# Cross-attention on one core: a new order of the first loads and products, and new costs and ranks in the planner

## The chip, the cores and the metric

The kernel runs on one core of a Trainium2 chip. The metric is the device time of one execution in microseconds. A core has TensorE (PE in the profile; PEld is its loading of weights), VectorE (DVE), ScalarE (ACT), GpSimd (POOL) and SyncE (SP), each with an instruction queue of its own that runs in the written order and waits on semaphores. SP issues nearly all DMA transfers here, POOL the indirect ones and some small loads. SBUF is the memory on the chip, PSUM the banks into which TensorE writes.

## What is computed

`x` is 2 x 2048 x 640, the context 2 x 128 x 384, all in float32. Cut to what matters:

```python
query = x @ Wq                                   # 8 heads of 80
hs = mha(query, enc @ Wk, enc @ Wv)              # enc: the context's first 124 rows
ca_q1 = einsum('btc,th->bch', ca, Wq_ca)[:, indices, :]   # ca: its last 4 rows
ca_hs1 = mha(ca_q1, x, x)                        # x is key and value
ca_q2 = ca_hs1 @ Wq
ca_hs2 = mha(ca_q2, ca @ Wk_ca, ca @ Wv_ca)
out = (hs + ca_hs2) @ Wout + b_out + x
```

`mha` is softmax attention with 8 heads. `indices` repeats 384 rows over 2048, so the second branch is worked out for 384 rows and gathered at the end.

## The kernel before, in words

The kernel is written by a small planner. Each stage is a Python generator that yields steps (`Do`): an engine, a function that emits the instructions, the events that it waits for, the buffers that it takes (`Room`) and frees. The `Desk` holds a queue of ready steps for each engine and a clock of its own. In `run` (from L167 on) it takes the step that can begin first by its estimate; among those that can begin at once it takes the lowest sum of rank and the price of a change of tile shape (`order` and `change`). What it emits is pinned in this order, so the estimate decides the order of every engine's queue, and nothing of it is left to the chip. The parts of the estimate are:

- `matmul` (L210), `transpose`, and `__getattr__` (L228), which prices a VectorE, ScalarE or GpSimd operation by its largest operand;
- `dma` (L254): an issue of 0.45 us, a transfer time given by the caller on one shared channel, and a tail, `more`, until the data can be used;
- the weights `SWITCH`, `LEAVE` and `ANOTHER` for going between whole 128x128 products and products on parts of the array (L70);
- `RANKS`, a table of offsets for single stages (block 3 of the chain of steps and so on), found by a search outside the kernel.

The work in order of time:

1. Head. `first_loads` loads the first 512 rows of `x` in four transfers of 128 rows (320 KB each), then Wq in five chunks. A chunk is 128 columns' worth of heads; the fifth gathers what is left between the others. `idle_work` multiplies zeros to keep TensorE going. `x_first` copies the fifth columns together on VectorE, transposes the rows on TensorE in groups of four tiles and lets ScalarE or VectorE copy each group to SBUF. `queries(0, ..., True)` then makes three of the five output chunks at once, in five parts, one for each chunk of Wq, each on all 512 rows; it begins when the whole of x's first block is there. The transposes, the zeros and the first query products share four PSUM banks; four more, the `quad`, wait for the adapter's scores.
2. Set-up. `keys`, `values_weights`, `text_values`, `y_weights`, `wq_turned` prepare the weights of both branches.
3. Per block of 512 rows (eight): `x_load`, `yz_block` and `y_rows` for the second branch; `queries_fast` for the query product, in a scheme of seven products of halves in place of eight, for which `sums_of_x` and `sums_of_wq` subtract tiles on POOL or VectorE; `halves_away` and `rest_back`, which carry the fifth chunk through DRAM (tiles `away`, `landing`, `rests`).
4. Per pair of 128-row tiles (16): `text_scores` (tile `sc`), `softmax` (maxima `m`, exponentials and product `p` with `r`, transposed `eb`), `probabilities` through DRAM (`kept`, `pT`), `text_out` (hidden `ph`, output `po`), added to `x_more` or `last_rows` and stored.
5. For each batch the `adapter`: scores `s`, their maxima `mx`, exponentials `ea`, contraction `acc`, then `second`, whose rows an indirect DMA gathers and adds at the end (`add_second`).

The lines that matter for the head:

```python
op = yield Do("PE", turn, [("xlast", (n0 + 3) // NCH)], needs=[(banks, 1)])      # x_first: four transposes
...
op = yield Do("PE", part, [*after, ("wq", i)])       # queries: after is [("x", 0, 0)], the whole block
```

Of the kernel before, what the change touches and what calls it, by code (L numbers as in the profile page):

```python
# [64 lines left out]
class Desk:  # L65
# [4 lines left out]
    WHOLE, SWITCH, LEAVE, ANOTHER = (P, P), 9.7, 11.5, -0.4  # L70
# [15 lines left out]
        "adapter": {1: 1},  # L86
        "chain": {8: -11, 9: -18, 11: 6, 12: -2, 14: -17, 15: -5, 17: 4, 18: 4, 19: 4, 20: 9, 24: -15, 37: -13,
            38: 4, 39: -8, 40: 8, 41: 3, 45: -13, 52: -5, 57: -2, 59: 10, 65: -8, 71: 11, 80: -12, 85: 9,
            87: -11},
        "context": {0: -12},  # L90
        "contract": {0: 5, 1: 12, 2: 12, 3: 9},
        "halves_away": {1: -6, 3: -10, 4: -8},
        "keys": {0: 4},
        "probabilities": {1: -2, 2: -4, 3: 7, 4: 1, 6: -1.4, 8: -4},
        "queries": {0: -4},
        "queries_fast": {3: 10, 4: 3},
        "rest_back": {8: 14, 9: 2},
        "softmax": {3: -7, 12: -11, 13: -2, 20: -18, 22: 6, 23: -14, 25: -3, 27: -12, 28: 6},
        "sums_of_wq": {0: 2},
        "text_scores": {3: -3, 6: 2, 11: 6, 12: 6, 14: 6},  # L100
        "text_values": {0: 8},
        "values_weights": {0: 6},
        "wq_turned": {0: 1},
        "x_load": {1: -12, 6: -6},
        "y_rows": {1: 2, 3: 10, 4: 1, 7: 8},
        "yz_block": {0: -13, 1: -4, 2: -2, 6: 5, 7: 2},
    }

    def __init__(self, tc):
        self.tc, self.nc, self.now, self.spent, self.mode = tc, tc.nc, 0.0, 0.0, None  # L110
        self.free = {e: 0.0 for e in self.ENGINES}
        self.queue = {e: [] for e in self.ENGINES}
        self.events, self.landed, self.channel, self.log, self.begun = {}, 0.0, 0.0, [], {}
# [114 lines left out]
    def __getattr__(self, name):  # L228

        side, _, what = name.partition("_")  # L230
        engine = {"v": self.nc.vector, "a": self.nc.scalar, "g": self.nc.gpsimd}[side]
        base, each = {"v": (0.06, 1.04), "a": (0.13, 0.77), "g": (0.1, 2.1)}[side]
        base += self.MORE.get(name, 0.0)

        def call(*args, **kw):
            self.pin(getattr(engine, what)(*args, **kw))  # L236
# [26 lines left out]
def kernel(  # L263
# [36 lines left out]
    FAST, SPARE, IDLE = 2, 0, 14  # L300
# [18 lines left out]
    ending, late = Room(1), {}  # L319
# [120 lines left out]
    def load_w(name, w, **kw):  # L440

        def go(at):
            w_c[name] = sp.tile([P, NCC, H], F32, tag=f"w{at[0]}", name=f"w_{name}")
            dma(w_c[name], w.rearrange("(c p) n -> p c n", p=P), 3.5)
            return at[0]

        return Do("SP", go, needs=[(weights, 1)], marks=[("w", name)], **kw)

    def first_loads():

        def whole(at):
            t = xrow.tile([P, 4 * H], F32, tag="xz", name="xz")
            rows_of[0] = t.rearrange("p (k n) -> p k n", k=4)

        yield Do("NONE", whole, [], needs=[(staging, 1)])
        for k in range(4):
            yield Do(
                "SP", lambda k=k: dma(rows_of[0][:, k], x[0, k * P : (k + 1) * P, :], (0.3, 0.9, 1.4, 1.1)[k], more=2.3), [],
                marks=[("xrows", k)],
            )  # L460
        for c in range(4):
            yield Do(
                "SP", lambda c=c: dma(wq_sb[:, c, :], Wq[D2 * c + VR : D2 * c + VR + P, :], 0.8), [],
                marks=[("wq", c)],
            )
            if c == 0:
                yield Do("SP", lambda: dma(wqca_sb, Wq_ca, 0.1), [], marks=["wqca"])
                yield Do("SP", lambda: dma(ctx_sb, enc.rearrange("b t c -> t b c"), 1.0), [], marks=["ctx"])
# [53 lines left out]
    def idle_work():  # L522
# [6 lines left out]
        op = yield Do("NONE", lambda at: (bank(at[0], "unread"), at[0]), needs=[(banks, 1)])  # L529
        to, at = op.value  # L530
        for n in range(IDLE):

            def product():
                matmul(to[:, :P], zeros, zeros, start=True, stop=True)

            yield Do("PE", product, [] if n else [op.at], frees=[(banks, at)] if n == IDLE - 1 else [])
# [30 lines left out]
    def x_first():  # L567
# [4 lines left out]
            "NONE", lambda s: slot(s[0], "xt_0_0", [P, 4, NCH, P]), [], needs=[(xslots, 1)]  # L572
        )
        xt[0, 0] = op.value, op.slots[0][0]
        flat = op.value.rearrange("p k c s -> p (k c s)")
# [6 lines left out]
        for n0 in range(0, 4 * NCH, 4):  # L582

            def turn(s, n0=n0):
                pt = bank(s[0], f"pt_x_{n0}")
                for n in range(n0, n0 + 4):
                    k, c = divmod(n, NCH)
                    src = rows_of[0][:, k, D2 * c + VR : D2 * c + VR + P] if c < 4 else last[:, k, :]
                    transpose(pt[:, n % 4 * P : (n % 4 + 1) * P], src, ident)
                return pt  # L590

            op = yield Do("PE", turn, [("xlast", (n0 + 3) // NCH)], needs=[(banks, 1)])
            end = n0 + 4 == 4 * NCH
            yield Fork(
                one(evacuate(
                    flat[:, n0 * P : (n0 + 4) * P], op.value, op.slots[0][0], after=[op.at],
                    marks=[("xpart", n0 // 4)],
                )), 1,
            )
        yield Do(  # L600
            "NONE", lambda: None, [("xpart", n) for n in range(NCH)],
# [311 lines left out]
    def load_wout():  # L913

        by_head = Wout.rearrange("(c j d) n -> j d c n", c=4, j=2)
        for j in range(2):
            yield Do(
                "SP", lambda j=j: dma(wout_sb[VH * j : VH * (j + 1), :4, :], by_head[j, :VH], 2.5),
# [132 lines left out]
    def x_load(b, sb, after):  # L1051
# [8 lines left out]
        for i in range(4):  # L1060
            part = slice(R * i, R * (i + 1))
            d0 = VR + R * i
            yield Do("SP", lambda: dma(most[part], v[:, :, :, d0 : d0 + R], 2.2, 1.3), [])
# [33 lines left out]
    def queries(n, after, first=False):  # L1097

        b, sb = divmod(n, NSB)
        yield Do("NONE", lambda: None, after)  # L1100
# [5 lines left out]
        if first:  # L1106
            yield Do("NONE", room, after, needs=[(qslots, 1)])
# [3 lines left out]
            for i in range(NCH):  # L1111

                def part(i=i):
                    for c in range(3):
                        matmul(
                            pq[c], wq_of(i, c), t[:, :, i, :], start=(i == 0), stop=(i == NCH - 1)
                        )

                op = yield Do("PE", part, [*after, ("wq", i)])
# [236 lines left out]
    def halves_away(n, pq, s, at, first=None):  # L1356

        away = away_of[n] = hbm.tile([P, 2, 512], F32, tag=f"rest_{n}", name=f"away_{n}")
        for k in range(2):
            cols, needs, frees = slice(2 * P * k, 2 * P * (k + 1)), [], []  # L1360
            if n:
# [9 lines left out]
                "SP", lambda k=k, z=z, cols=cols: dma(away[:, :, cols], z.bitcast(F32), 0.6), [op.at],  # L1371
# [34 lines left out]
    def yz_block(b, sb):  # L1406
# [35 lines left out]
        for u in range(2):  # L1442
# [10 lines left out]
            if b:  # L1453
                yield Do(
                    "SP", lambda u=u: dma(away[:, u], zs, 1.0), frees=[(zss, i)],
# [32 lines left out]
    def y_rows(b, sb):  # L1488
# [3 lines left out]
        for u in range(2):  # L1492
# [11 lines left out]
            def away(t=op.value, u=u):  # L1504
                dma(kept[:, :, u, :], t.rearrange("p (a n) -> p a n", a=4), 1.0)
# [179 lines left out]
    def second(b):  # L1685
# [12 lines left out]
        def less():  # L1698
            for ct in range(NCC):
                desk.v_tensor_reduce(  # L1700
# [43 lines left out]
        for ct in range(NCC):  # L1744
            op = yield Do("NONE", lambda e: ea_tile(e[0], f"o2_{b}_{ct}"), [here], needs=[(eas, 1)])
            o2, k = op.value.rearrange("p g k -> p (g k)")[:, :H], op.slots[0][0]
            for u in range(2):
# [16 lines left out]
                "SP", lambda: dma(o2_of[b][ct * P : (ct + 1) * P, :], o2, 1.3),  # L1764
# [64 lines left out]
    def softmax(m, k, sc, s, i, at):  # L1829
# [59 lines left out]
    def probabilities(m):  # L1889
# [9 lines left out]
        for j in range(4):  # L1899
            op = yield Do(  # L1900
                "SP",
                lambda: dma(pT[R * j : R * (j + 1)].rearrange("p i k h a -> p i (k h a)"), by_keys[j], 1.1),
# [76 lines left out]
    def residual(m):  # L1979

        xr = xr_of[m] = []
        for b, st in tiles(m):

            def load(at):
                t = row_of[at[0]]
                dma(t, x[b, st * P : (st + 1) * P, :], 1.3)
# [12 lines left out]
    def add_second(t, b, st):  # L1999
# [6 lines left out]
        desk.spent += 1.9  # L2006
        desk.landed = desk.now + desk.spent + 6.5
# [149 lines left out]
    def stored(m, k, both):  # L2157
# [5 lines left out]
        if gather_last[m] and not desk.known(("o2", b)):  # L2163
            part = hbm.tile([P, H], F32, tag=f"early_{m}_{k}", name=f"early_{b}_{st}")
            op = yield Do("SP", lambda: dma(part, t, 1.3), both, frees=[(rows, i)])
            yield Do("NONE", lambda: None, [op.at, ("o2", b)])

            def load(at, _):
                t = row_of[at[0]]
                dma(t, part, 1.3)  # L2170
# [8 lines left out]
        yield Do("SP", lambda: dma(rows_out, t, 1.3), both, frees=[(rows, i)] + own)  # L2179
# [11 lines left out]
    begin = desk.begin  # L2191
    desk.free["POOL"] = 12.0
    begin(idle_work(), 9)
# [57 lines left out]
```

## Time and profile before

| | us |
|---|---|
| median of 3 runs | 603.02 (602.94 to 606.83) |
| the profiled execution, its own time | 603.33 |
| its span, first to last instruction | 601.6 |
| TensorE busy | 583.4 |
| VectorE busy | 405.0 |
| ScalarE busy | 280.7 |
| GpSimd busy | 152.3 |
| end of the last product in the timeline | 597.9 |

A row of a group names the line, the engine, the operation, what it writes and reads, its shape and its count; L211, L221, L236 and L256 are lines of helpers, so groups are told apart by their tiles. A row of waits gives the total, the number and the longest. In the chain of work that ended last each piece is followed back to what released it. In a table of stretches the columns are the stretch, its length, the busy time of PE, PEld, DVE, ACT and POOL with the number of instructions, TensorE's granted clock (1.00 throughout), the DMA engines' busy share and GB/s. One float32 product of a 512-row tile is two instructions.

### The profile page before, as it was taken

How to read it: one execution, taken by the hardware profiler on the slowest of the kernel's cores; microseconds unless marked ns; L12 is line 12 of the kernel's file. 1: busy time of each engine (PE TensorE's matmuls, PEld its weight loads, DVE VectorE, ACT ScalarE, POOL GpSimd, SP SyncE). 2: the span in 40 equal slices, each digit the busy share in tenths (PEclk: the TensorE clock that was granted, in tenths of full speed). 3: DMA queues.
4: the chain of work that ended last, by engine and by line, in shares of the span. 5: the costliest groups of instructions: out<-in, count | busy, mean ns of one | idle time of the engine just before them, and what ended most of it. 6: DMA issues, size and time to landing. Idle time of an engine off the chain costs nothing.

```text
span 601.6 us, 11824 instructions
## 1 busy us (share of the span) xinstructions
PE 583.4 (97%) x4535; PEld 362.8 (60%) x4535; DVE 405.0 (67%) x642; ACT 280.7 (47%) x766; POOL 152.3 (25%) x203
## 2 busy tenths in 40 slices
PE   9999989999999999999999999999999999999997
PEld 6475455856757755465665566656555556666764
DVE  2257698989999977465989999998412243344343
ACT  2233156455445589799735252346865831102010
POOL 7201021413222330100204252534022202124242
PEclk9999999999999999999999999999999999999999
DMA  8998825965769586454898789896673794699997
GB/s 276 176 244 172 137 83 168 178 185 168 131 169 210 151 156 190 151 160 141 182 277 231 190 194 292 221 257 157 192 169 60 173 261 100 220 226 295 213 256 185
DMA packets 153106, 114.21 MB, mean 190 GB/s; under 512 B 83285, under 2 KB 125653, under 8 KB 153050
## 3 DMA queue, kind: packets, MB, share of 16 engines
q1 hardware_dynamic: 147418, 102.77, 66.2%
q0 software_dynamic: 5632, 10.69, 10.7%
q8 instruction: 36, 0.59, 0.4%
q14 instruction: 20, 0.16, 0.1%
HBM read 72.22 MB, written 41.21 MB: 189 GB/s over the span
## 4 chain that ended last, share of the span: by engine, by line
PE 61%; DVE 19%; DMA 8%; ACT 6%; issue 3%; SPq 1%; DVEq 0%; ACTq 0%
PE po L211 22%; PE pq L211 13%; PE ph L211 6%; DVE mx L236 6%; PE acc L211 5%; PE s L211 4%; PE sc L211 4%; DMA pT<-kept 3%; ACT ea L236 3%; ACT p L236 2%; DVE m L236 2%; DMA zb<-z 2%; DVE eb L236 2%; DMA kept<-eb 2%; PE pyz L211 2%
## 5 line engine op out<-in xcount | busy, mean ns | idle before, releaser
L236 DVE TENSOR_REDUCE mx<-s 128x4 f32<-128x2048 f32 x48 | 109.1, 2272 | 8.5 <-PE s L211 8.5
L236 ACT ACTIVATE ea<-s 128x2048 f32<-128x2048 f32 x48 | 91.9, 1915 | 23.8 <-PE s L211 23.5
L236 ACT ACTIVATE p<-sc,m 128x124 f32<-128x124 f32 x256 | 90.9, 395 | 24.4 <-DVE m L236 24.1
L211 PE MATMUL pq<-xt,wq_sb 128*128 128x256 f32 (+1 forms) x272 | 86.4, 452 | 2.5 <-DVE q L236 2.3
L211 PE MATMUL po<-wout_sums,hs 128*128 128x320 f32 x256 | 79.3, 441 | 0.4 <-DVE x_more L236 0.4
L211 PE MATMUL po<-wout_sb,hs 128*128 128x320 f32 x248 | 77.0, 440 | 0.0
L236 DVE TENSOR_TENSOR x_more<-x_more,po 128x320 f32<-128x320 f32 x80 | 38.3, 480 | 56.2 <-PE po L211 54.0
L211 PEld LDWEIGHTS pq<-xt,wq_sb 128*128 128x128 f32 x272 | 48.9, 190 | 28.4 <-issue 18.5
L236 POOL TENSOR_TENSOR p<-p,r 128x992 f32<-128x992 f32 x18 | 33.3, 1848 | 124.4 <-DVE r L236 124.4
L211 PEld LDWEIGHTS po<-wout_sums,hs 128*128 128x128 f32 x256 | 46.6, 190 | 24.5 <-issue 5.1
L236 ACT ACTIVATION_READ_ACCUMULATOR p<-sc,m 128x1 f32 x256 | 60.0, 238 | 0.0
L211 PEld LDWEIGHTS po<-wout_sb,hs 128*128 128x128 f32 x248 | 45.5, 190 | 23.2 <-issue 4.3
L236 ACT COPY hs<-ph 128x512 f32<-128x512 f32 (+1 forms) x34 | 18.7, 551 | 74.8 <-PE ph L211 74.8
L2001 POOL DMA_INDIRECT x_more<-o,query x20 | 32.5, 1626 | 77.1 <-DVE x_more L236 60.9
L211 PE MATMUL acc<-ea,y_sb 128*32 128x384 f32 (+2 forms) x768 | 51.4, 385 | 0.0
L211 PE MATMUL ph<-pT,vpad 128*32 128x256 f32 x768 | 46.3, 381 | 2.9 <-DMA pT<-kept 2.0
L236 DVE TENSOR_REDUCE m<-sc 128x4 f32<-128x496 f32 x64 | 40.0, 660 | 13.1 <-PE sc L211 13.0
L236 DVE TENSOR_TENSOR last_rows<-last_rows,po 128x320 f32<-128x320 f32 x48 | 23.2, 485 | 31.4 <-PE po L211 30.8
L236 ACT CAST rests<-landing 128x512 fp32r<-128x512 f32 x30 | 19.4, 648 | 45.5 <-PE sc L211 42.8
L236 DVE STREAM_TRANSPOSE eb<-p 128x1024 f32<-128x1024 f32 x32 | 39.3, 1229 | 1.8 <-DMA kept<-eb 1.6
L211 PEld LDWEIGHTS sc<-kmain,q 64*128 64x128 f32 x512 | 31.8, 187 | 14.2 <-issue 8.8
L211 PE MATMUL pq<-xt,wq 128*128 128x512 f32 x80 | 39.8, 612 | 0.0
(210 smaller groups left out, 798.4 us busy)
## 6 DMA issues: line engine op xcount, KB each, us to landing
kept<-eb SPq DMA_DIRECT2D x32, 512.0 KB, 3.9
pT<-kept SPq DMA_DIRECT2D x64, 256.0 KB, 7.2
landing<-away SPq DMA_DIRECT2D x60, 128.0 KB, 3.5
xi<-in_x_dram SPq DMA_DIRECT2D x28, 256.0 KB, 4.8
x_more<-in_x_dram SPq DMA_DIRECT2D x20, 320.0 KB, 3.9
out_dram<-x_more SPq DMA_DIRECT2D x20, 320.0 KB, 5.5
y<-yt SPq DMA_DIRECT2D x16, 256.0 KB, 3.6
y_sb<-y SPq DMA_DIRECT2D x32, 128.0 KB, 4.1
```

Source lines behind the costliest of these rows:

```text
L211: self.pin(self.nc.tensor.matmul(out, lhsT, rhs, **kw))
L236: self.pin(getattr(engine, what)(*args, **kw))
L2001: desk.pin(nc.gpsimd.indirect_dma_start(out=t, out_offset=None, in_=o2_of[b], in_offset=bass.IndirectOffsetOnAxis(ap=query[:, st : st + 1] ...
```

## The change

The first loads alternate: x rows 0, x rows 1, Wq 0, Wq 1, x rows 2, x rows 3, Wq_ca, the context, Wq 2, Wq 3. The first four banks of the transposes and of the products of zeros become a tile of the `quad` (`early`), which is given back when x's first block is there. `x_first` transposes the four main tiles of one row group as soon as its rows have landed, and the fifth tiles of two row groups together. `queries(0)` makes the parts of Wq 0 and Wq 1 on 256 rows each, first half before second. The products of zeros go from 14 to 10. All else is in the planner: other transfer times and tails, a charge for VectorE operations with two tiles in SBUF that begin while POOL is at work, other weights for changes of shape, a start of 0.8 us for four engines, and a new table of ranks. The diff, cut to its core:

```diff
-    WHOLE, SWITCH, LEAVE, ANOTHER = (P, P), 9.7, 11.5, -0.4
+    WHOLE, SWITCH, LEAVE, ANOTHER = (P, P), 10.9, 10.2, -2
...
-        "softmax": {3: -7, 12: -11, 13: -2, 20: -18, 22: 6, 23: -14, 25: -3, 27: -12, 28: 6},
+        "softmax": {3: -7, 9: 0.2, 10: 14, 12: -11, 13: -4, 18: -18, 19: -7, 20: -2, 25: -3, 28: 6},
...
+        def both(what, args):
+            if what not in ("tensor_tensor", "scalar_tensor_tensor"):
+                return False
+            pair = (args[1], args[2] if what == "tensor_tensor" else args[3])
+            return all(a.space == bass.MemoryType.SB and a.shape[-1] * a.shape[1] >= 96 for a in pair)
...
+            if side == "g":
+                self.port = self.now + self.spent
+            elif side == "v" and both(what, args) and self.port > self.now:
+                self.spent += min(self.port - self.now, 0.9)
...
-    def dma(self, out, in_, us, issue=0.45, more=2.8):
+    def dma(self, out, in_, us, issue=0.45, more=1.5):
...
-    FAST, SPARE, IDLE = 2, 0, 14
+    FAST, SPARE, IDLE = 2, 0, 10
...
+        yield x_rows(0, 0.3)
+        yield x_rows(1, 0.9)
+        yield chunk(0, 1.3, more=2.3)
+        yield chunk(1, 1.1, more=2.3)
+        yield x_rows(2, 1.1)
+        yield x_rows(3, 1.1)
+        yield Do("SP", lambda: dma(wqca_sb, Wq_ca, 0.1, more=2.3), [], marks=["wqca"])
+        yield Do("SP", lambda: dma(ctx_sb, enc.rearrange("b t c -> t b c"), 1.0, more=2.3), [], marks=["ctx"])
+        yield chunk(2, 0.9, more=2.3)
+        yield chunk(3, 0.9, more=2.3)
...
+    def early_banks():
+        op = yield Do("NONE", lambda s: late_sq.tile([P, 4, 512], F32, tag="sq", name="early"), [], needs=[(quad, 1)])
+        early.tile = op.value
+        early.at += [0.0] * 4
+        yield Do("NONE", lambda s: None, [("x", 0, 0)], needs=[(early, 4)], frees=[(quad, 0)])
...
+        for h in range(2):
+            k0 = 2 * h
+            for n, part in enumerate((
+                [(k0, c) for c in range(4)], [(k0 + 1, c) for c in range(4)], [(k0, 4), (k0 + 1, 4)],
+            )):
...
+            for i, h in ((0, 0), (1, 0), (0, 1), (1, 1), *((i, None) for i in range(2, NCH))):
+                u = slice(0, 4) if h is None else slice(2 * h, 2 * h + 2)
...
-            dma(kept_of[m][:, :, k], eb.rearrange("p j h a -> p j (h a)"), 2.1)
+            dma(kept_of[m][:, :, k], eb.rearrange("p j h a -> p j (h a)"), 1.6)
...
-        desk.spent += 1.9
-        desk.landed = desk.now + desk.spent + 6.5
+        desk.spent += 1.0
+        desk.landed = desk.now + desk.spent + 6.3
...
+    for e in ("PE", "ACT", "DVE", "SP"):
+        desk.free[e] = 0.8
```

The tables of the other stages' ranks change in the same way, and the other transfers: loads of weights 3.5 to 2.6, `x_load` 2.2 to 1.5, rows in and out 1.3 to 0.9, `pT` 1.1 to 1.15 with a tail of 1.9, the parts of Wout 2.5 to 1.8; `away` of the rests goes up, 0.6 to 0.8, `y` 1.0 to 1.5.

More of the change, by code (lines that the diff above doesn't have):

```diff
@@ L318 @@
     yts = Room(2)
-    ending, late = Room(1), {}
+    ending, early, late = Room(1), Room(0), {}
     def bank(i, name):
@@ L527, in idle_work @@
         yield Do("DVE", lambda: desk.v_memset(zeros, 0.0), [])
-        op = yield Do("NONE", lambda at: (bank(at[0], "unread"), at[0]), needs=[(banks, 1)])
-        to, at = op.value
+        op = yield Do("NONE", lambda at: at[0], needs=[(early, 1)])
+        to, at = early.tile[:, op.value], op.value
         for n in range(IDLE):
@@ L581, in x_first, with turn @@
             )), 1)
[L582 to L599, printed above, removed]
+        for h in range(2):
[3 more added lines that the diff above has]
+            )):
+                def turn(s, part=part):
+                    pt = early.tile[:, s[0]]
+                    for i, (k, c) in enumerate(part):
+                        src = rows_of[0][:, k, D2 * c + VR : D2 * c + VR + P] if c < 4 else last[:, k, :]
+                        transpose(pt[:, i * P : (i + 1) * P], src, ident)
+                    return pt
+                op = yield Do(
+                    "PE", turn, [("xrows", k0 + n)] if n < 2 else [("xlast", k0), ("xlast", k0 + 1)],
+                    needs=[(early, 1)],
+                )
+                to = xt[0, 0][0][:, k0 + n, :4] if n < 2 else xt[0, 0][0][:, k0 : k0 + 2, 4]
+                src = op.value[:, : len(part) * P].rearrange("p (c s) -> p c s", s=P)
+                yield Fork(one(Do(
+                    EITHER, lambda to=to, src=src: copy(to, src), [op.at], frees=[(early, op.slots[0][0])],
+                    marks=[("xpart", h, n)],
+                )), 1)
         yield Do(
-            "NONE", lambda: None, [("xpart", n) for n in range(NCH)],
+            "NONE", lambda: None, [("xpart", h, n) for h in range(2) for n in range(3)],
             frees=[(first_rows, at), (staging, 0)], marks=[("x", 0, 0)],
@@ L2178, in stored @@
             both = [op.at]
[L2179 removed]
+        yield Do("SP", lambda: dma(rows_out, t, 0.9), both, frees=[(rows, i)] + own)
     blocks = [(b, sb) for b in range(B) for sb in range(NSB)]
```

97 lines of the change are left out of this document (49 added, 48 removed).

## The prediction, made before the result was known

> **What bounds the kernel now.** I read the page's totals first, then the busy time by stretches, then what TensorE waited for, then the chain that ended last, and last the first ten microseconds and the DMA issues. The totals:
>
> ```profile
> PE 583.4 (97%) x4535; PEld 362.8 (60%) x4535; DVE 405.0 (67%) x642; ACT 280.7 (47%) x766; POOL 152.3 (25%) x203
> ```
>
> TensorE has work for all but 18.2 us of the 601.6 us span. By stretches (length, then busy time of PE, PEld, DVE, ACT and POOL):
>
> ```profile
> 0.00:9.50 9.50, 8.15 (x54) 7.48 (x54) 2.90 (x17) 3.53 (x5) 8.53 (x47) 1.00 0.80 271
> 9.50:75.00 65.50, 65.50 (x346) 35.17 (x346) 34.02 (x80) 15.61 (x41) 10.64 (x46) 1.00 0.92 191
> 75.00:180.00 105.00, 101.29 (x654) 66.10 (x653) 98.88 (x131) 54.60 (x207) 27.82 (x20) 1.00 0.63 154
> ...
> 500.00:601.70 101.70, 97.94 (x590) 65.46 (x588) 41.93 (x89) 11.61 (x24) 28.31 (x18) 1.00 0.89 219
> ```
>
> From 9.5 to 75 us TensorE never rests, so a product that starts earlier moves everything up to 75. From 75 to 180 VectorE is busy 94% of the time and TensorE 96%: two engines bind there at once. The last 100 us are products without a gap and a store behind them. What TensorE waited for, in total, times, longest:
>
> ```profile
> PE pq L211 <- DVE q L236: 4.4, 4, 1.6
> PE ph L211 <- DMA pT<-kept: 2.0, 2, 1.2
> PE s L211 <- DVE mx L236: 1.6, 4, 0.6
> PE s L211 <- ACT ea L236: 1.2, 4, 0.7
> PE pt_p L221 <- DVE p2pad L236: 1.1, 1, 1.1
> PE unread L211 <- DVE zeros L236: 1.1, 1, 1.1
> ```
>
> All rows of that answer add to 13.9 us, 1.3 of them in the head (zeros 1.1, x's rows 0.2). So 12.6 us is all that another order could take out of visible waits; VectorE is named for most of it, DMA for only 2.0. Four pieces of the chain explain some of it (start, length, what):
>
> ```profile
> 78.34 1.44 DVE x_sums L236
> 79.78 2.81 DVE wq_sums L236 x2
> ...
> 149.46 1.56 DVE zop L236
> ...
> 325.98 1.63 DVE wout_sums L236
> ```
>
> The groups show what is odd about them (min/median/max in ns):
>
> ```profile
> L236 DVE TENSOR_TENSOR wq_sums<-wq_sb x2: 384/934/1485, 77.3 to 79.7; 128x256 f32<-128x256 f32 x2
> L236 DVE TENSOR_TENSOR wq_sums<-wq_sums,wq_sb x2: 409/947/1485, 81.1 to 84.3; 128x256 f32<-128x256 f32 x2
> L236 DVE TENSOR_TENSOR x_sums<-xt x1: 1519/1519/1519, 78.3 to 78.3; 128x512 f32<-128x512 f32 x1
> ```
>
> The same instruction takes 384 ns or 1485 ns. In the timeline every slow one starts while POOL runs a subtraction or product of two tiles.
>
> **The change, part by part. The head.** SP now issues x rows 0, x rows 1, Wq 0, Wq 1, x rows 2, x rows 3, then Wq_ca, the context, Wq 2 and Wq 3: the same bytes in the same number of issues. Landings go by place in the queue, so I take them from the old occupants. The first landed 3.0 us after its issue at 0.81, at 3.8; the third let VectorE and TensorE go at 6.57 to 6.59; the fourth at 7.72; the fifth (Wq 0, issued at 2.66, 6.0 to landing) at 8.66; the next 320 KB I put 1 us later, at 9.7. Before, the first useful product stood behind all 20 transposes of x and those of Wq_ca:
>
> ```profile
> 9.47 2.84 PE L211 MATMUL pq<-xt,wq_sb 128*128 128x512 f32 x6
> 12.14 0.38 PE L221 MATMUL pt_ctx<-ident,ctx_sb 128*128 128x128 f32 x2
> ```
>
> After it, the products of Wq 0 with half of the rows start when Wq 0 lands, at 6.6 (the transposes of x rows 1, landed before 5.1, and a copy of 0.59 end by 6.4). Each half part is six instructions at half the 0.43 us of a 512-row one, 1.3 us; the two run from 6.6 to 9.2, the second fed by Wq 1 at 7.7. Then come ten transposes at 0.11 (1.1 us), those of Wq_ca (0.5), and the rest of the first five parts: five parts of 2.57 us are 12.85, less 2.6 done, 10.25, with three pairs of context transposes at 0.22, 0.66. That ends at 6.6 + 2.6 + 1.1 + 0.5 + 10.25 + 0.66 = 21.7, plus a gap for x rows 3: landing 9.7, transposes, a copy of 0.6, so 10.8 against 9.2 + 1.1 + 0.5 already filled, 0 to 0.6. Before, the chain has the same work end at 9.54 + 2.77 + 0.22 + 2.58 + 0.22 + 2.58 + 0.22 + 5.15 = 23.3, some 0.2 of it modelled drain, so 23.1. The gain lies between 0.8 and 1.4, and below that if TensorE's written order stands in front of a late landing: down to -0.3. I take 0.9. It is hidden by nothing up to 75; Wq 2 (needed at about 13.5, landed at 12) and the later loads keep their places, the ninth issue still waiting for the first landing. Fewer idle products (10 for 14) cost nothing: they fill the wait before x's rows, which is still there. The early tile of four banks takes over the transposes' banks until x's first block is done, long before the first scores at 52 us need them; its price is nothing, and 0.4 (one bank's evacuation) if that block's last copy is late.
>
> [...]
>
> **VectorE's collisions.** The estimate now charges a two-tile VectorE operation that begins while POOL is busy. Excess in the rows: wq_sums 2 x (1485 - 409) = 2.15 us; x_sums 1519 - 684 = 0.84; the zop row at 149.38, 1.65 against 0.73, 0.92; wout_sums 1714 against some 820 (by the slope from 409 at 256 to 684 at 512 elements), 0.89; 4.8 us together, all four on the chain. What TensorE gets back is bounded by its own waits behind them: 1.60 at 84.41, 0.69 at 156.91, and 0.43 + 0.58 behind the maxima at 329.87 and 339.89, so 3.3 seen, and up to the 4.8 if the 94% busy VectorE passes the rest on. The other end is nothing: the planner may dodge by letting POOL start later. I take 3.0, near the visible waits. With VectorE early, the next limit at 84 us is the softmax's maxima behind the first scores.
>
> [...]
>
> **The other constants and the ranks.** They add no instruction; they decide the order on each queue. DMA terms shrink. Issue 0.45, transfer and tail together, old, new and measured:
>
> ```profile
> kept<-eb SPq DMA_DIRECT2D x32, 512.0 KB, 3.9
> pT<-kept SPq DMA_DIRECT2D x64, 256.0 KB, 7.2
> landing<-away SPq DMA_DIRECT2D x60, 128.0 KB, 3.5
> ...
> y_sb<-y SPq DMA_DIRECT2D x32, 128.0 KB, 4.1
> ```
>
> kept: 5.35, 3.55, 3.9; landing: 3.95, 2.65, 3.5; y_sb: 3.65, 2.35, 4.1 (four in a row share the channel). The old terms were late by 0.5 to 1.5, the new ones are early by 0.4 to 1.7. The indirect gather goes from 1.9 to 1.0, where the tail shows five starts 1.85 apart. The weights for a change of tile shape shift by about 1 among ranks that differ by 10; one costs about 0.19 (in the chain, eight pq products take 1.92 between other shapes and 1.73 between their like), and with three or four kinds of small products, 48 pieces of acc the most regular of them, ten more or fewer are 1.9 us either way, which I set at nothing. For the new ranks as such the trace gives bounds: all remaining visible waits gone, 12.6 - 3.3 = 9.3 us gained; or every one of the 15 landing groups 0.85 too early for its scores, 12.8 us lost. I take nothing between them, as the estimate errs by the same size on either side.
>
> **The sum.** The profiled execution took 603.33 us (span 601.6 and 1.7 around it), 0.3 over the median of 603.02. 603.33 - 0.9 - 3.0 = 599.4; against the median, 599.1 us.
>
> **Rivals.** (1) Slower: the plan runs early. TensorE's queue is in written order; scores stand behind rests, rests behind landing<-away, and if the scores are placed 0.85 us before their data can be there, each of the 15 groups stalls everything behind it. Eleven of 15 give 9.4: 603.0 - 0.9 - 3.0 + 9.4 = 608.5. It decides from five groups on (4.6 x 0.85 = 3.9). For it: the new terms are below every measured landing above. Against it: only 2.0 us of DMA waits today, with rests given out well ahead. (2) Deeper: with waits charged truly, the search removes half of the 9.3 us that is left: 599.1 - 4.7 = 594.4. For it: VectorE's waits have a name and a price now, and the old terms held transfers back. Against it: with PE and DVE both at 94% and over in 75 to 180, filling one wait opens another. (3) Nothing but the head: the collisions move instead of going, 603.0 - 0.9 = 602.1. For it: POOL's subtractions need the same tiles at the same time as VectorE's.
>
> **How the numbers follow.** Forecast 599.1 (range 596 to 602): 0.33. Deeper: 0.27. Head only: 0.14. Slower: 0.26. About 1%, 6 us, is what a measurement of this kernel tells from no change. Under 597.0 lie 0.24 of the deeper case and 0.07 of the forecast, 0.31; over 609.0 lie 0.19 of the slow one; the other 0.50 is within. The range, from the deeper case with nearly all 9.3 us (590) to the slow one with 11 groups and half a microsecond (609), leaves out 0.2.
>
> **What would show it.** In the head: the first product of x and Wq at 6.6 instead of 9.47, and the first five parts done about 0.9 earlier. Collisions: wq_sums all near 400 ns, no x_sums over 700, no wait of TensorE behind q at 84. The slow rival: TensorE's wait on landing or pT above 5 us, or ACT's rests named before sc. Deeper: the waits of TensorE together below 8 us. I am wrong if those waits stay as they are and the time still moves: then changes of shape or hidden stalls inside the products decide, which the busy time does not show.

## The result, and the profile after

| | us |
|---|---|
| before, median of 6 runs | 604.24 (601.87 to 607.49) |
| after, median of 6 runs | 623.58 (622.42 to 625.57) |
| ratio | 1.0318, 95% interval 1.0278 to 1.0358 |
| after, the profiled execution; its span | 623.33; 621.6 |

The change makes the kernel 3.2% slower; 599.1 was forecast, and the range ended at 609. The profiled span grew by 20.0 us. The same stretches as before, up to the longer end (stretch, its length, busy time of PE, PEld, DVE, ACT, POOL, then granted clock, DMA share, GB/s):

```profile
0.00:9.50 9.50, 7.02 (x28) 6.07 (x28) 1.41 (x7) 2.45 (x3) 8.53 (x47) 1.00 0.78 266
9.50:75.00 65.50, 60.66 (x328) 36.66 (x327) 26.12 (x88) 15.92 (x39) 10.45 (x46) 0.95 0.86 181
75.00:180.00 105.00, 103.42 (x654) 64.21 (x653) 102.14 (x128) 51.39 (x195) 27.83 (x21) 1.00 0.69 165
...
350.00:500.00 150.00, 141.40 (x1324) 84.85 (x1323) 91.29 (x133) 77.04 (x194) 46.34 (x38) 0.98 0.80 202
500.00:621.70 121.70, 112.56 (x749) 72.96 (x747) 44.68 (x99) 22.68 (x33) 31.76 (x24) 1.00 0.78 199
```

The row of before for 350 to 500 us:

```profile
350.00:500.00 150.00, 147.00 (x1415) 86.22 (x1408) 89.99 (x143) 79.22 (x167) 41.15 (x34) 1.00 0.80 196
```

Set these beside the stretches shown before. TensorE now rests 1.6 us in 75 to 180, against 3.7: the middle got better. But it rests 4.8 us in 9.5 to 75, where it never had, 8.6 in 350 to 500 (3.0 before) and 9.1 in the last stretch (3.8). Over the span TensorE's rests grew from 18.2 to 30.6, 12.4 us. Its busy time grew from 583.4 to 591.0, 7.6 us, with four product instructions more among 4539 (twelve from the halves, eight fewer of zeros): nearly the same work ran slower, and two rows show a clock under 1.00. What TensorE waited for:

```profile
PE s L210 <- DVE mx L242: 5.2, 2, 3.9
PE ph L210 <- DMA pT<-kept: 3.2, 2, 2.3
PE pt_vca L220 <- ACT vca L242: 3.2, 1, 3.2
PE po L210 <- DVE last_rows L242: 2.7, 1, 2.7
PE po L210 <- POOL hs L242: 1.6, 1, 1.6
...
PE early L220 <- ACT xt L242: 1.4, 2, 0.7
```

Before, the longest single wait was 1.6 us. Now a few long ones stand there, most of them behind operations whose instructions the change leaves as they were.

To place the loss I counted every product at a fixed time by its shape in both traces, and read when each kernel had done the same amount of TensorE's work. After is 5.7 us behind at 22 us, 4.6 at 59, 11.5 at 82. It then catches up to 5.0 at 355. It is 11.0 behind at 378, 14.9 at 433, 14.1 at 595 and 18.9 at its last product. So the middle gained 6.5 us, and four places lost more: the head, 62 to 72, 355 to 433, and the tail.

**The head.** TensorE's timeline of after, with the wait in brackets:

```profile
8.80 0.80 PE L210 MATMUL early<-zeros 128*128 128x128 f32 x2 [0.68 <-ACT xt L242]
10.11 0.80 PE L210 MATMUL early<-zeros 128*128 128x128 f32 x2 [0.52 <-DVE xt L242]
10.70 4.20 PE L210 MATMUL pq<-xt,wq_sb 128*128 128x256 f32 x12
```

Products of zeros wait for copies of x. They have nothing to do with x, but they are written into the tile `early`, and so are the transposes; a write into one of its banks waits for the copy out of another (e1 below takes this away). The first useful product begins at 10.7, not at 6.6, though Wq 0 landed at 6.8, near the forecast. The twelve take 4.2 us, 0.35 apiece.

**62 to 72 us.** ScalarE's and then TensorE's timeline:

```profile
63.56 1.02 ACT L242 CAST krest<-k_parts 128x992 fp32r<-128x992 f32 x1 [6.83 <-DMA k_parts<-k_away]
...
65.63 0.35 ACT L242 COPY vca<-pvca 128x128 f32<-128x128 f32 x2
```

```profile
65.95 0.47 PE L220 MATMUL pt_vca<-ident,vca 128*128 128x128 f32 x1 [3.19 <-ACT vca L242]
```

ScalarE stands in written order at the cast of `krest` until its transfer lands, the copy of `vca` is written behind it, and TensorE stands behind that. Then the clock falls (a stretch of two microseconds; the third number from the end is the granted clock):

```profile
66.00:68.00 2.00, 2.00 (x11) 1.17 (x12) 2.00 (x4) 0.58 (x1) 0.00 (x0) 0.50 0.56 151
```

**355 to 433 us.** VectorE, and TensorE behind it:

```profile
367.16 1.25 DVE L242 STREAM_TRANSPOSE eb<-p 128x1024 f32<-128x1024 f32 x1 [4.75 <-DMA kept<-eb]
368.32 0.16 DVE L242 RECIPROCAL r<-r 128x8 f32<-128x8 f32 x1
368.41 2.24 DVE L242 TENSOR_REDUCE mx<-s 128x4 f32<-128x2048 f32 x1
```

```profile
370.70 0.50 PE L210 MATMUL s<-zop,cop 32*128 32x512 f32 x4 [3.93 <-DVE mx L242]
```

`eb` has one buffer. Its store was issued at 357.05 and landed 10.0 us later, where the median of that group is 3.9. VectorE waits 4.75 for it, the maxima `mx` stand behind, and TensorE's scores behind them.

The late landing itself is not new. In before, the chain that ended last and VectorE's timeline have the same store at this place:

```profile
355.70 11.01 DMA kept<-eb
```

```profile
356.20 2.28 DVE L236 TENSOR_REDUCE mx<-s 128x4 f32<-128x2048 f32 x1
...
360.44 2.29 DVE L236 TENSOR_REDUCE mx<-s 128x4 f32<-128x2048 f32 x1
...
363.76 2.29 DVE L236 TENSOR_REDUCE mx<-s 128x4 f32<-128x2048 f32 x1
366.81 1.25 DVE L236 STREAM_TRANSPOSE eb<-p 128x1024 f32<-128x1024 f32 x1 [0.76 <-DMA kept<-eb]
```

It landed 11.0 us after its issue, with the DMA engines' busy share at 1.07 meanwhile (1.08 in after from 357 to 367). But VectorE had three reductions `mx` written between the store and the next `eb`, reached `eb` 10.3 us after the store's issue and waited 0.76. In after, one `mx` stands there, and VectorE reaches `eb` after 5.4 us. The transfers are as late in both kernels; the new order comes for the buffer 5 us sooner.

**The collisions** are what the change did mend:

```profile
L242 DVE TENSOR_TENSOR wq_sums<-wq_sb x2: 384/631/878, 78.9 to 79.8; 128x256 f32<-128x256 f32 x2
L242 DVE TENSOR_TENSOR wq_sums<-wq_sums,wq_sb x2: 427/664/900, 81.7 to 82.6; 128x256 f32<-128x256 f32 x2
...
L242 DVE TENSOR_TENSOR x_sums<-xt x1: 710/710/710, 200.1 to 200.1; 128x512 f32<-128x512 f32 x1
```

The slow `wq_sums` went from 1485 to 878 and 900, not to the 400 forecast, and the wait behind `q` at 84 is gone. The slow `zop` and `wout_sums` are gone too: the longest now take 752 and 895 ns. The row of `x_sums` is another instruction, at 200 us: of nine that VectorE had on `x`'s tiles one is left, the others went to GpSimd (15 before, 23 after). There the longest takes 2291 ns, against 1594 before. So the planner took work off VectorE (405.0 us busy before, 389.6 after) and let part of the collisions fall on GpSimd.

### The profile page after: what moved, and what is told of

It reads as the page before. It is cut to its first block, busy times and chain, and to the rows that moved or that the text cites. A ratio compares the mean times of both kernels' runs of the same rounds, so it can differ in the third digit from the quotient of the medians.

```text
span 621.6 us, 11860 instructions
## 1 busy us (share of the span) xinstructions
PE 591.0 (95%) x4539; PEld 370.2 (60%) x4539; DVE 389.6 (63%) x627; ACT 283.5 (46%) x769; POOL 168.2 (27%) x216
## 3 DMA queue, kind: packets, MB, share of 16 engines
q0 software_dynamic: 5632, 10.69, 10.3%
## 4 chain that ended last, share of the span: by engine, by line
PE 45%; DVE 23%; DMA 15%; SPq 7%; issue 4%; ACT 3%; POOL 1%; POOLq 0%; DVEq 0%; ACTq 0%
PE po L210 20%; DVE mx L242 8%; SPq L266 7%; PE pq L210 6%; PE ph L210 5%; DMA kept<-eb 5%; PE acc L210 4%; DMA pT<-kept 3%; PE s L210 3%; DVE xt L242 3%; PE sc L210 2%; DVE eb L242 2%; DVE m L242 2%; DMA zb<-z 2%; DVE q L242 2%
## 5 line engine op out<-in xcount | busy, mean ns | idle before, releaser
L210 PE MATMUL pq<-xt,wq_sb 128*128 128x256 f32 (+1 forms) x284 | 91.1, 456 | 2.7 <-DVE wq_sums L242 1.1
L210 PE MATMUL po<-wout_sb,hs 128*128 128x320 f32 x240 | 75.1, 441 | 1.6 <-POOL hs L242 1.6
L210 PEld LDWEIGHTS pq<-xt,wq_sb 128*128 128x128 f32 x284 | 52.4, 197 | 27.4 <-issue 17.1
L242 DVE TENSOR_TENSOR x_more<-x_more,po 128x320 f32<-128x320 f32 x68 | 32.2, 480 | 51.3 <-PE po L210 51.2
L210 PEld LDWEIGHTS po<-wout_sb,hs 128*128 128x128 f32 x240 | 43.9, 190 | 23.7 <-issue 5.1
L2039 POOL DMA_INDIRECT x_more<-o,query x17 | 26.8, 1577 | 114.8 <-DVE x_more L242 89.4
L242 ACT ACTIVATION_READ_ACCUMULATOR p<-sc,m 128x1 f32 x256 | 55.9, 218 | 0.0
L242 DVE TENSOR_TENSOR last_rows<-last_rows,po 128x320 f32<-128x320 f32 x60 | 28.8, 482 | 42.6 <-PE po L210 35.2
L242 ACT COPY hs<-ph 128x512 f32<-128x512 f32 (+1 forms) x37 | 20.4, 556 | 64.8 <-PE ph L210 64.8
L242 DVE STREAM_TRANSPOSE eb<-p 128x1024 f32<-128x1024 f32 x32 | 39.6, 1237 | 11.6 <-DMA kept<-eb 11.5
L210 PE MATMUL sc<-kmain,q 64*128 64x124 f32 x512 | 38.4, 287 | 1.4 <-DVE last_rows L242 1.4
```

What stands on the lines that cost most here:

```text
L210: self.pin(self.nc.tensor.matmul(out, lhsT, rhs, **kw))
L2039: desk.pin(nc.gpsimd.indirect_dma_start(out=t, out_offset=None, in_=o2_of[b], in_offset=bass.IndirectOffsetOnAxis(ap=query[:, st : st + 1] ...
```

## The experiments

Theory at the start: three stalls of the new order, each with a name, make the loss (T: the one tile in the head; S: ScalarE behind `krest`; and the crowd of transfers near 355, which makes `kept` land late). Rival F: the order as a whole is at fault. The written order is tuned to one set of charges; any other order has stalls of its own, and to take one away only shows the next. All ratios are to the kernel before in the same job.

| kernel | median us | ratio, 95% |
|---|---|---|
| after | 623.58 | 1.0318, 1.0278 to 1.0358 |
| e1_four_tiles | 619.92 | 1.0254, 1.0222 to 1.0285 |
| e2_krest_pool | 613.78 | 1.0165, 1.0095 to 1.0235 |
| e4_tiles_krest | 612.40 | 1.0145, 1.0078 to 1.0212 |
| e6_k_first | 610.58 | 1.0117, 1.0057 to 1.0177 |
| e9_mended; e9b_mended_again | 613.33; 612.63 | 1.0158, 1.0106 to 1.0209; 1.0141, 1.0110 to 1.0173 |
| e14_fewer_rows | 608.45 | 1.0091, 1.0061 to 1.0120 |
| e3_kept_back | 646.89 | 1.0746, 1.0678 to 1.0813 |
| e5_kept_act | 629.37 | 1.0413, 1.0349 to 1.0477 |
| e7_all | 624.54 | 1.0328, 1.0260 to 1.0395 |
| e8_before_kept | 616.21 | 1.0221, 1.0147 to 1.0295 |
| e10_old_ranks | 629.08 | 1.0401, 1.0335 to 1.0466 |
| e11_before_new_ranks | 629.45 | 1.0419, 1.0363 to 1.0475 |
| e12_before_head | 615.61 | 1.0176, 1.0125 to 1.0227 |
| e13_no_head | 616.52 | 1.0208, 1.0176 to 1.0239 |

### Taking the stalls of the changed kernel away

**e1_four_tiles**: the same order, with `early` made of four PSUM tiles.

```diff
-        op = yield Do("NONE", lambda s: late_sq.tile([P, 4, 512], F32, tag="sq", name="early"), [], needs=[(quad, 1)])
+            return [pool.tile([P, 512], F32, tag=f"e{i}", name=f"early_{i}") for i in range(4)]
```

> The changed kernel with the same written order on every queue; only the four early banks are four PSUM tiles in place of one. Theory T (the shared tile makes products, zeros and copies of different banks wait for each other, and the broken stream also keeps the clock low): the first product of Wq starts at 6.8 to 7.5 us in place of 10.7, the clock is full before 8 us in place of 13.6, the first five parts end near 22 us in place of 26.4, and the time falls by 4 to 6 us, to 617 to 619. Rival C (10 products of zeros in place of 14 are too few to raise the clock, whatever the tiles): the first products run at 0.35 us an instruction as before, full clock after 12 us, and the time stays at 621 or more.

TensorE's timeline:

```profile
7.10 2.83 PE L210 MATMUL pq<-xt,wq_sb 128*128 128x256 f32 x12
...
22.45 2.55 PE L210 MATMUL pk<-ctxT,k 128*128 128x256 f32 x6 [2.06 <-DVE k L242]
```

The waits on x's copies are gone and the first twelve products begin 3.6 us earlier and run at 0.24 us apiece. So the one tile made the head's waits. But most of this is given back: the loads land when they did, so TensorE now waits 2.06 us for Wk, the next 3.4 us run at a granted clock of 0.50, and the wait behind `krest` grows from 3.2 to 5.9. At 82 us the kernel is 11.4 behind, as after was. The median, 619.92, lies just outside the 617 to 619 expected. The profiled execution, 622.86, is the slowest of the four, so the trace does not show where the median gained its 4 us.

**e2_krest_pool**: the same order as after, the cast of `krest` on GpSimd.

```diff
-            "ACT", lambda: copy(krest.rearrange("p g b k -> p g (b k)"), parts),
+            desk.pin(nc.gpsimd.tensor_copy(krest.rearrange("p g b k -> p g (b k)"), parts))
```

> The changed kernel with the same written order, but the rounding copy of the keys' rest (krest) is done by GpSimd at its place in the plan in place of ScalarE, so that yz and vca no longer stand behind it on ScalarE's queue. Theory S (TensorE's 3.2 us wait at 62.8 is this queue, and the half clock from 64.8 to 71.6 follows from the wait): the wait goes, the clock stays full through 75 us, and the time falls by 5 to 7 us, to 616 to 618. Rival (the wait only moves, because z and the first scores stand behind the same late transfers): the clock may stay full, but less than 2 us is gained, 621 or more.

The wait behind `vca` is gone, and the kernel is 2.9 behind at 74 us. The gain of some 9 us is more than the 5 to 7 expected, and about 3 of it are not the cast's (at 22 us it is 2.7 behind, not 5.7): in the profiled execution the same head, with the same waits of 0.68 and 0.52, runs its twelve products in 2.75 us, not 4.20. The crowd stays: TensorE waits 4.3 us behind `mx` near 361.

**e4_tiles_krest**: both edits at once.

> The four tiles and the copy of krest on GpSimd together, in the changed kernel's written order. If the two losses are separate places on TensorE's path (T and S), the gains add: 10 to 13 us, 610 to 613. If an earlier head only makes the stop at 62 us longer, because that stop ends when a transfer lands, the sum is no better than the krest run alone, 616 to 618.

612.40 lies in the range expected if the gains add, but it is no proof: the single gains in ratio, 0.6% and 1.5%, would make 2.2% together, 1.7% came, and the ratio of e2 alone, 1.0165, is within the interval of e4. The wait for Wk is 2.7 us here, and the granted clock is 0.74 in 20 to 25 us and 0.91 in 25 to 30.

**e6_k_first**: e4 with Wk loaded before Wk_ca (theory W: what comes next is Wk).

```diff
-        kca = yield load_w("kca", Wk_ca, after=[])
-        k = yield load_w("k", Wk, after=[])
+        kca = yield load_w("kca", Wk_ca, slot=1, given=("k", Wk), after=[])
+        k = yield load_w("k", Wk, slot=0, given=("kca", Wk_ca), after=[])
```

> The four tiles and krest on GpSimd (e4) with the loads of Wk_ca and Wk exchanged in SyncE's queue, nothing else moved. In e1 and e4 the earlier head ran into the product pk, written ahead of other products because the plan has Wk landed before 20 us, while it landed at 20 to 21.7 us: 2.1 to 2.7 us of wait and 3.4 us of half clock. Theory W (a transfer charged too short, on the path): Wk lands near 17.5 us, the wait at 22.5 and the half clock to 26 go, TensorE is 3 to 4.5 us earlier at 60 us than in e4, and the time is 608 to 610 against 612.4. Rival: later waits for transfers (krest, pT) take it back, 611 to 614.

The wait for Wk is gone. The step from e4, 0.3% in ratio, is within the intervals; it is the trace that shows the repair. This order is now 0.4 us ahead of before at 22 us and 7.65 ahead at 343. Then the crowd comes (3.5 us behind `mx` at 357.6; the granted clock, 1.00 in every stretch up to 75, is 0.990 over the span), and at the last product it is 6.0 behind. Three repairs together took 12 of the 19 us; the whole remaining loss in this trace, 13.6 us from 343 on, is the end of the order.

**e9_mended**: e6 with the last pair's subtractions on VectorE; e9b_mended_again is the same kernel in another job.

> The kernel with the four early tiles, krest's cast on GpSimd and Wk ahead of Wk_ca (610.58), with the last pair's subtractions on VectorE in place of GpSimd, and nothing else. If TensorE's 1.6 us wait on those subtractions near the end is worth its length: 608 to 609.5. If the last row load, which made TensorE wait 1.5 us there, ends the stretch anyway: 610 to 611.

> The mended kernel once more, beside the one with fewer rows, to compare both in one job: the same written order, so 610 to 614 by the first measurement.

The wait of 1.6 us on `hs` is gone and the time is not lower: 613.33 and 612.63. Taking that wait out of the tail gained nothing that can be measured. An earlier wait of the tail, for VectorE's `last_rows`, grew from 1.5 to 2.1 us; VectorE stands there at the load of the last rows of x. That is the second case, though the time is above its 610 to 611.

### The crowd near 355 us

**e3_kept_back**: after, with the old charge for the store of `kept`.

```diff
-            dma(kept_of[m][:, :, k], eb.rearrange("p j h a -> p j (h a)"), 1.6)
+            dma(kept_of[m][:, :, k], eb.rearrange("p j h a -> p j (h a)"), 2.1, more=2.8)
```

> The changed kernel with one constant pair of before: the store of eb (kept) is charged 2.1 and 2.8 us again in place of 1.6 and 1.5; the planner makes a new order from it. Theory K (the short charge lets VectorE's next transposition be written before its only buffer is free, 11.5 us of waits on kept in place of 1.6, and the maxima and TensorE's scores stand behind it): those waits fall below 4 us, TensorE's wait on mx below 2 us, and the time falls by 4 to 8 us, to 615 to 619. Rival R (the ranks were searched for the new charges, so that any other order is worse): VectorE's waits on kept fall, but the time is 622 or more.

VectorE's waits on `kept` fall from 11.5 to 5.0 us, and yet this is the worst kernel of all, as rival R has it: the one number moves steps everywhere, and waits of 4.2 (`p2pad`), 3.5 (`mx`) and 2.7 us (`q`) appear.

**e5_kept_act**: e2 with these stores issued from ScalarE's queue, in case SP's queue held them.

```diff
-        self.pin(self.nc.sync.dma_start(out, in_))
+        self.pin((queue or self.nc.sync).dma_start(out, in_))
```

> The krest run (e2) with the same written order, but the 32 stores of eb (kept) are issued from ScalarE's queue in place of SyncE's. Theory Q (a store of eb lands up to 10 us after its issue because it stands behind other transfers of SyncE's queue, VectorE's next transposition waits for the only eb buffer, and TensorE's 4 us wait for mx near 361 us with the half clock behind it is that): kept's longest landing falls from about 10 to 5 us or less, VectorE's waits on it from 11 to below 4 us, the half clock near 361 to 368 goes, and the time falls from 613.8 by 5 to 7 us, to 607 to 609. Rival (the DMA engines themselves are full, whichever queue issues): the landings and waits stay, and the time stays at 612 to 616.

VectorE still waits 10.5 us in all on `kept` (12.0 in e2), and the store issued at 357.75 lands 11.6 us later. SP's queue was not the cause of the late landing. TensorE's longest wait behind `mx` falls to 1.8 us all the same: VectorE reaches that `eb` only 9.3 us after the store's issue. The time is worse than the rival expected, with new waits elsewhere; the longest, 4.0 us at 161, is for ScalarE, which stood there 7.2 us at a load of `landing`, and why that is late stays open. **e7_all** adds the same queue and e9's subtractions to e6, and loses what e6 had won:

> All the mended places in the changed kernel's written order: four tiles, krest on GpSimd, Wk first, kept from ScalarE's queue, and in the last pair of tiles the subtractions that the plan gives to GpSimd (behind five gathers 1.85 us apart that it has at 1.0) done on VectorE. If the losses are the named waits and the half clock behind them, 14 to 18 us of the 19.6 come back: 605 to 609. If the order as such costs (more changes of tile shape, later transfers), it stays above 611.

**e14_fewer_rows**: the order of e9, with three row transfers of 128 rows near 337 to 341 cut to 16 rows and one memset added. It leaves out 336 rows of loads, so its output is not the kernel's.

```diff
-                dma(t, x[b, st * P : (st + 1) * P, :], 0.9)
+                n = 16 if m == 2 else P
+                dma(t[:n], x[b, st * P : st * P + n, :], 0.9)
...
-                dma(t, part, 0.9)
+                n = 16 if m == 5 else P
+                dma(t[:n], part[:n], 0.9)
```

> The mended kernel (613.33 in its job, profiled span 608.1) in the same written order, with three row transfers near 337 to 341 cut to their first 16 of 128 rows (the loads of unit 2's two row tiles and the reload of unit 5's), so that those rows hold other data; one memset on GpSimd beside it. If the store of kept there lands 10.3 us after its issue because the transfers' engines are full: 0.84 MB less, some 3 us at 270 GB/s, so it lands after 7 to 8 us, TensorE's wait of 3.94 us behind mx at 359 falls under 1.5, and the time falls by 2.5 to 5 us. If the store is late for another reason: landing still 9.5 or more and the wait still 3 or more.

VectorE in e9b_mended_again and then in this kernel:

```profile
359.19 1.25 DVE L242 STREAM_TRANSPOSE eb<-p 128x1024 f32<-128x1024 f32 x1 [4.81 <-DMA kept<-eb]
```

```profile
354.37 1.25 DVE L242 STREAM_TRANSPOSE eb<-p 128x1024 f32<-128x1024 f32 x1 [1.95 <-DMA kept<-eb]
```

TensorE in the same two kernels:

```profile
362.73 0.80 PE L210 MATMUL s<-zop,cop 32*128 32x512 f32 x4 [3.98 <-DVE mx L242]
```

```profile
357.91 0.51 PE L210 MATMUL s<-zop,cop 32*128 32x512 f32 x4 [1.35 <-DVE mx L242]
```

Fewer bytes take 4.2 us off the time (608.45 against 612.63 in the same job) and the wait behind `mx` falls under 1.5, as the crowd has it. But the landing fell only from some 9.6 us to 8.6, not to 7 or 8; the rest of the shorter wait is VectorE itself, which came to `eb` 6.7 us after the store's issue in place of 4.9. So a shorter crowd helps, and so does a VectorE that comes later. But before has the crowd too, with the landing of 11.0 us shown above, and loses 0.8 us of VectorE's time to it. What the change added is how soon VectorE wants the buffer. No run moved that one step alone or gave `eb` a second buffer.

### One part of the change alone

**e8_before_kept**: before, with only the shorter charge for `kept`.

> The kernel before with one charge alone changed in its planner, the store of eb at 1.6 and 1.5 us in place of 2.1 and 2.8 as in the change; no instruction is added or left out, the order alone is made anew with the old ranks. Theory F (ranks and charges fit only together, and any single new charge spoils the order): 615 us or more. Rival (the short charge for kept is one of the losses by itself but the rest of the order holds): 604 to 611, with VectorE's waits on kept up from 1.6 us.

**e10_old_ranks**: e4 with the table of ranks of before. **e11_before_new_ranks**: before with the new table alone.

> The changed kernel with the four early tiles and krest's cast on GpSimd (612.40), its charges kept, but the table of ranks of the kernel before. If the search of ranks belongs to one set of charges and the old table is merely another order with the new charges: 615 or more. If the new table is the fault: 608 or less.

> The kernel before with the new table of ranks alone, its charges and its head kept. If a table fits only the charges that it was searched with: 615 or more, with new waits of TensorE above 2 us. If the new ranks by themselves carry the gain of the middle of the changed kernel: 604 or less.

**e12_before_head**: before with the new head alone, in four tiles.

> The kernel before, its charges and ranks kept, with the new head alone (alternating loads, first products on 256 rows, ten idle products, four early tiles). If the head is worth what was forecast and the order after it survives: near 602 to 603. If the planner makes another order behind the new head and that order has waits of its own: 610 or more.

**e13_no_head**: before with all new charges and ranks, but its own head.

> The kernel before with all new charges and the new ranks, but its own head. If the loss of the change lies in its head (the one tile of four banks, Wk late, krest late): 598 to 603, since the middle of the changed kernel gained 6.5. If charges, ranks and head fit only together, so that any part alone makes an order with waits of its own: 612 or more, with at least one wait of TensorE above 3 us that neither kernel has.

All five end where F put them in time, 11 to 25 us over before. In e8 one number, for a transfer that is charged 1.8 us less, costs 13 us; its profiled execution keeps up with before until 350 and then has waits of up to 2.0 us. In e12 the head does no harm, with 0.0 lag at 22 us, but the order behind it is another, and TensorE meets this:

```profile
159.08 0.80 PE L212 MATMUL s<-zop,cop 32*128 32x512 f32 x4 [7.20 <-DVE mx L244]
```

e13 says where the 355 stall belongs. It has the charges and ranks, not the head, and it has the same wait: 4.1 us behind `mx` at 364. So that stall comes with the charges and ranks; my expectation that e13 would show a wait that neither kernel has was wrong, its largest new one is 1.5. VectorE reaches `eb` 5.3 us after the store's issue there, as in after. Without the new head the kernel costs 2.1%, with it 3.2%. The wait behind `vca` at 62 is in neither e12 nor e13: it takes the head and the charges together.

What follows for F: no part is good by itself, and the parts do not add. Yet F in its strong form falls too: e6 shows that named repairs stick, 12 us of them. That each table was found by a search for one set of charges, and fits no other, is what these five runs suggest; the search itself was not run.

## Why the prediction was wrong, step by step

- **Collisions, -3.0.** The mechanism was right as far as the rows show: the four slow operations on VectorE are shorter or gone, and the middle, 82 to 355, gained 6.5 us. Not all of it need be the collisions': the planner also moved eight `x_sums` to GpSimd, and no run has the charge for collisions alone. "Two engines bind there at once" held: time given back to VectorE came out at TensorE.
- **The head, -0.9.** Wrong in "its price is nothing", with 0.4 if the last copy is late. I looked at which banks `early` takes over and when it gives them back, and not at what one tile of four banks does to the waits between them. At 22 us the changed kernel was 5.7 behind, some 3 us of it slow products (0.35 us apiece) that e2 with the same head does not have. With four tiles the head gains 0.4 (e6) or 0.0 (e12) at 22 us, so the forecast of the loads was about right and that of the end too high.
- **"From 9.5 to 75 us TensorE never rests, so a product that starts earlier moves everything up to 75."** The premise was read from the old order. The new one rests 4.8 us there. Work that is pulled ahead meets loads that did not move: Wk and `krest` are late next. I had named Wq 2 and looked no further.
- **The other constants and the ranks, 0.** This is the step that failed. e13, which has all charges and ranks and the old head, ends 13.2 us over before, where the terms for charges and ranks gave -3.0. From 355 on the changed kernel lost 13.9 us in waits and slow clock (0.50 in 372 to 374, 0.57 in 416 to 420); at 62 to 72 it lost 7 more, behind a ScalarE order that neither the head alone (e12) nor charges and ranks alone (e13) made. I had bounds of -9.3 and +12.8 and took the middle "as the estimate errs by the same size on either side". But here the loss of an order had no symmetry. Errors did not cancel along a queue in written order: `eb`, which came 5 us early, bought nothing, and stopped `mx` and TensorE's scores behind it. Five kernels with other orders all ended 1.8% to 4.2% over before.
- **The slow rival** had the right sign by the wrong road. TensorE's waits on `landing` are none and those on `pT` 3.2 us, under the 5 that I asked for. What ran early was not the scores but VectorE's `eb` on `kept`, one of the three charges that I had tabled as too short (3.55 against 3.9). I had compared it with the median; at the place that counts the landing took 11.0 us in before already, in the chain of the profile that I read. Nor were all old terms late: `y_sb` was charged 3.65 and took 4.1, and `pT`, charged 4.35, took 7.2.
- **The bound on waits.** "12.6 us is all that another order could take out" was a bound for gains only. For losses I took one mechanism at 0.85 us apiece; single waits of 3 to 4 us were not in it, nor the granted clock of 0.50 that came with two of them (65 to 71 with that of 3.19 us, 372 to 374 behind that of 3.93); TensorE's busy time grew by 7.6 us here.

Settled by runs: the one tile, Wk, and `krest`, together 12 us; singly, only that of `krest` is well clear of the intervals. Shown by the traces, but not by a run that changes this alone: that the stall near 355 comes with VectorE's earlier step and not with later transfers. Open: what the slow clock and the later waits add up to 433, and the 4.8 us of the tail. Of its two waits the one that was removed gained nothing; the longer one, 2.73 us behind the load of the last rows of x, was not tried.

## What to carry to other kernels

Where a planner's estimate fixes every queue's order, a new charge is a new kernel: price it by the orders that it can make, with more room on the slow side, and not by the error that it corrects. Compare a charge with the slowest landing at the place where a queue waits, and not with the median of its group. When a stage starts earlier, list the next three loads that it will meet. A scratch tile of several banks shared by steps that have nothing to do with each other made them wait for each other here (0.68 and 0.52 us in the head, gone in e1); give each bank its tile.

## What the runs showed of the hardware

A slow clock came with a wait of TensorE of 2.06 and one of 3.19 us, and in these two places the loss was about twice the wait, an estimate from the stretches. In after, with the 3.19 us wait that began at 62.8, the granted clock was 0.50 from 65 to 71 (0.91 in the microsecond before, 0.68 in the one after); in e1 a wait of 2.06 us was followed by 3.4 us at 0.50 and then 0.99. In e2, where the wait behind `vca` is gone, the clock is 1.00 from 62 to 75, against 0.74 in after. Not every wait has it: with the 2.73 us in after's tail the clock is 1.00 from 596 to 606. What decides it was not shown.

Nor was the cause of what I had not expected in the head: the same instructions and waits, with twelve products in 4.20 us in one kernel (after; they start 0.43 us apart up to 13.3 and 0.21 apart from 13.7) and 2.75 in another (e2). The granted clock reads 1.00 in both stretches, so the low clock of e1's Theory T and Rival C does not show in it.

A store's landing is no constant: `kept`, 512 KB, landed in 3.9 us by the median, in 10.0 (after) and 11.0 (before) where the engines' share was 1.08 and 1.07, so no single charge can be right for it.
